# The autocorrelation's shifted sums: two circles of 128 steps in place of one of 255

## The chip, the cores and the metric

The kernel runs on one core of a Trainium2 chip, all in float32. The metric is the device time of one execution in microseconds (us). A profile is one execution seen by the hardware profiler; its times are counted from the first instruction of that execution.

## The reference, cut to what matters

The program is a two-layer decoder for 8 sequences of 128 tokens with 512 features. Layer 0 is causal attention, an autocorrelation with a second input (the context), and a feed-forward part with low-rank experts; layer 1 has attention, cross-attention and another feed-forward part. Each sublayer ends in a residual and a normalization. The change is in layer 0's autocorrelation, whose keys and values are both the context:

```python
qf = jnp.fft.fft(q, axis=2)
kf = jnp.fft.fft(k, axis=2)
corr = jnp.fft.ifft(qf * jnp.conj(kf), axis=2).real
topk = int(C * np.log(L))                       # 9 of 128 shifts, per feature
w, idx = jax.lax.top_k(corr.transpose(0, 1, 3, 2), topk)
w = jax.nn.softmax(w, axis=-1)
for i in range(topk):
    g = jnp.minimum(idx[:, :, None, :, i] + pos, L - 1)
    out = out + w[:, :, None, :, i] * jnp.take_along_axis(v, g, axis=2)
```

So for each feature there is a correlation over 128 shifts on a circle, a choice of the nine largest with softmax weights, and a sum of the values shifted by those amounts. A shift does not wrap round here: past the end, the last token is repeated.

## The kernel before, in words

Batch elements go through layer 0 in four pairs. Causal attention runs in 16 steps `n` (four pairs times four groups of heads, `f`). A step computes scores (`s_a`, line 165), adds the mask (`e_a`, line 370), takes maxima (`m_a`) and exponentials (line 194, ScalarE), turns the probabilities of the step before (`pt_a`, `pT_a`), multiplies out the step before that (`o_a`) and makes the next step's queries and keys (`pq`, `pk`). The output projection of a finished pair (`projection`, `po`) is spread over steps of the next.

The autocorrelation of a pair is the class `Correlated`, cut into pieces:

- `spectra`: real transforms of the tokens (`pa`) and the context (`pb`) by matmul with a table, 64 frequencies by cosine and sine; the two elements of the pair take 64 output partitions each. ScalarE copies pa to `xa`; VectorE multiplies (`pr`), GpSimd adds.
- `correlate`: back to 128 shifts (`pc`), copied to `co`.
- `chosen(h)`: for element `h` of the pair, the nine largest per feature by max and match_replace on VectorE (`top`, `nxt`, `wk1`, `wk2`), softmax weights `ex`.
- `shifted(h)`: the weights are turned (`pt_wT`, `wT`); the context (`pvf`) and the weights (`pw`) go to the spectrum of a circle of 255, long enough that no shift wraps; ScalarE copies pw to `wf`; VectorE forms the products (`vw`), GpSimd their sum and difference.
- `done(h)`: back to 128 positions (`poc`), residual and normalization.

The pieces of pairs 0 and 1 are laid into attention steps by the dictionary `beside`, beginning with step 7 for pair 0 and step 11 for pair 1, at two places in each step (`auto(n, 0)`, `auto(n, 1)`). Pair 2 begins after the last attention step; its rest, and pair 3, lie among the expert stage's pieces by an order written out by hand at lines 716 to 761 (`T`, `R` and `E` turn tokens, route them, and sum the experts). A scheduler puts the instructions on each engine, so the order on an engine is close to the text but not the same. Each engine works through its own queue in order.

PSUM is handed out by two pools: `bank` (four single banks) and `banks` (two double ones). The score and turning tiles of attention, and pa, pb, pc, pvf and pw, are double ones. Context tiles (`ct`) have four buffers, filled by `context(p)` on SP's queue: pairs 0 and 1 at the start, the others at the end of steps 11 and 15. The transform tables lie side by side in one tile, `dft`; T_A is the 128-circle, T_V and T_W the 255-circle of the context and of the weights, T_I and T_J the ways back.

Of the kernel before, what the change touches and what calls it, by code (L numbers as in the profile page):

```python
# [29 lines left out]


C_CAUSAL, C_HEAD = 0, 3 * P
C_SIGN = 3 * P + 2
N_MASK = 3 * P + 3
T_A, T_I, T_W, T_V, T_J = 0, P, 3 * P, 5 * P, 7 * P
N_DFT = 9 * P


# [5 lines left out]
def decoder(ctx: ExitStack, tc: tile.TileContext, a: dict, out: bass.AP):  # L44
# [15 lines left out]
    def banks(name):  # L60
        return ps2.tile([P, 2, 512], F32, tag="ps2", name=name)
# [17 lines left out]
    causal = masks[:, C_CAUSAL : C_CAUSAL + 3 * P]  # L79
    pair = masks[:, C_HEAD : C_HEAD + 2]  # L80
    sign = masks[:, C_SIGN : C_SIGN + 1]

    def mm_acc(ps, pairs):
        n = len(pairs)
# [222 lines left out]

    def context(p):
        for b in (2 * p, 2 * p + 1):
            cts[b] = cp.tile([P, D], F32, tag="ct", name=f"ct_{b}", bufs=4)  # L310
            nc.sync.dma_start(cts[b], a["ctx"][b])

    wq, wq_parts = by_columns("L0_Wq")
# [17 lines left out]
        xs[b] = xp.tile([P, D], F32, tag="x", name=f"x_in_{b}")  # L331
        nc.sync.dma_start(xs[b], a["x"][b])
    nc.sync.dma_start(dft, a["dft"])
    for p in range(2):
        context(p)
    wbase = weight4("F0_base")
    wlora = weight("F0_lora")
    w1q = weight4("L1_Wq")
# [30 lines left out]
    def causal_bias(e, s, r0):  # L369
        return nc.vector.tensor_tensor(e, s, bc(causal.unsqueeze(1), [P, 2, 3 * P]), ALU.add)  # L370

    def projection(b, oT):
        po = bank(f"po0_{b}")
        mm_acc(po, [(oT[:, b % 2, c, :], wo[:, c, :]) for c in range(NC)])
        nc.gpsimd.tensor_tensor(xs[b], xs[b], bqkv[:, 1, :], ALU.add)
        xs[b] = add_norm(xs[b], po, f"a0_{b}", late)


    def swapped(t):

        return t[:, 1:3, :]

    class Correlated:
# [5 lines left out]
        def spectra(self):  # L389

            ps = {}
            for n, src in (("a", xs), ("b", cts)):
                ps[n] = banks(f"p{n}_{self.p}")
                for i in range(2):
                    for h, b in enumerate(self.bs):
                        nc.tensor.matmul(
                            ps[n][64 * h : 64 * h + 64, i, :],
                            lhsT=dft[:, T_A + 64 * i : T_A + 64 * i + 64], rhs=src[b], start=True, stop=True,
                        )
                if n == "a":  # L400
                    xa = cp.tile([P, 3, D], F32, tag="sp", name=f"xa_{self.p}", bufs=2)
# [23 lines left out]
        def chosen(self, h):  # L425

            b, co = self.bs[h], self.co[:, h]

            top = sm.tile([P, NC, 8], F32, tag="top", name=f"top_{b}")
            nxt = sm.tile([P, NC, 8], F32, tag="nxt", name=f"nxt_{b}")  # L430
            wk1 = cp.tile([P, NC, P], F32, tag="wk1", name=f"wk1_{b}")
            wk2 = cp.tile([P, NC, P], F32, tag="wk2", name=f"wk2_{b}")
            for i in range(NC):
                nc.vector.max(top[:, i, :], co[:, i, :])
                nc.vector.match_replace(wk1[:, i, :], top[:, i, :], co[:, i, :], BIG)
                nc.vector.max(nxt[:, i, :], wk1[:, i, :])

            nc.vector.memset(nxt[:, :, TOPK - 8 :], BIG)
            for i in range(NC):
                nc.vector.match_replace(wk2[:, i, :], nxt[:, i, :], wk1[:, i, :], BIG)  # L440
# [3 lines left out]
            nc.vector.scalar_tensor_tensor(ex, wk2, BIG, ex, ALU.is_equal, ALU.mult)  # L444
            su = sm.tile([P, NC], F32, tag="su", name=f"su_{b}")
            nc.vector.tensor_reduce(su, ex, AX.X, ALU.add)
            rc = sm.tile([P, NC], F32, tag="rcw", name=f"rcw_{b}")
            nc.vector.reciprocal(rc, su)
            nc.gpsimd.tensor_tensor(ex, ex, bc(rc.unsqueeze(2), [P, NC, P]), ALU.mult)
            self.ex[h] = ex  # L450

        def shifted(self, h):
            b = self.bs[h]
            wT = cp.tile([P, NC, P], F32, tag="wT", name=f"wT_{b}")
            transposed(self.ex[h].rearrange("p c t -> p (c t)"), NC, P, wT, f"wT_{b}", "a")
            pv = banks(f"pvf_{b}")
            pw = banks(f"pw_{b}")
            for i in range(2):
                nc.tensor.matmul(
                    pv[:, i, :], lhsT=dft[:, T_V + i * P : T_V + (i + 1) * P], rhs=cts[b], start=True, stop=True  # L460
                )
# [11 lines left out]
            nc.vector.tensor_tensor(vw[1], pv, swapped(wf), ALU.mult)  # L473
            nc.gpsimd.tensor_tensor(vw[1][:, 0, :], vw[1][:, 1, :], vw[1][:, 0, :], ALU.subtract)
            self.ri[h] = [t[:, 0, :] for t in vw]

        def done(self, h):
# [22 lines left out]
    beside = {}  # L500
    for p in range(2):
        for i, pieces in enumerate(autos_of[p].pieces()):
            beside.setdefault((begun + NC * p + i // 2, i % 2), []).extend(pieces)

    def auto(n, place):
        for piece in beside.pop((n, place), []):
# [8 lines left out]
    for n, (p, f) in enumerate(steps):  # L515
# [215 lines left out]
    E(1)  # L731
    T(3)
    third.done(1)
    fourth.correlate()
# [1 line left out]
    fourth.chosen(0)  # L736
    E(2)
    T(4)
    R(4)
    fourth.shifted(0)  # L740
    fourth.chosen(1)
# [2 lines left out]
    xT = turned_tokens(0)  # L744
    fourth.done(0)
    R(5)
    E(4)
    fourth.shifted(1)
    raw = [normed(i, 0, xT) for i in range(2)]
# [443 lines left out]
def _mask_table():  # L1193
# [3 lines left out]
    t[:, C_CAUSAL : C_CAUSAL + 3 * P] = np.concatenate([half, half])  # L1197
    t[:, C_HEAD : C_HEAD + 2] = (np.arange(P)[:, None] // HD) % 2 == np.arange(2)
    t[:, C_SIGN] = np.where(np.arange(P) % 64 == 0, -1.0, 1.0)
    return t  # L1200


# [11 lines left out]
def _dft_table():  # L1214
# [10 lines left out]
    cos, sin = waves(S, s, f)  # L1225
    cos[:, 0], sin[:, 0] = even, odd
    t[:, T_A : T_A + 64], t[:, T_A + 64 : T_A + P] = cos, sin
    cos, sin = waves(S, f, s)
    cos[0], sin[0] = even, odd
    for n, part in enumerate((cos, sin)):  # L1230
        t[:, T_I + n * P :][:, :P] = np.concatenate([2 * part / S] * 2)

    n = 2 * S - 1
    cos, sin = waves(n, np.arange(n), s)
    t[:, T_W : T_W + P], t[:, T_W + P : T_W + 2 * P] = cos[:S], sin[:S]
    for i, whole in enumerate((cos, sin)):

        t[: S - 1, T_V + i * P :][:, :P] = whole[: S - 1]
        t[S - 1, T_V + i * P :][:P] = whole[S - 1 :].sum(0)
    c = np.where(s == 0, 1.0, 2.0)[:, None] / n  # L1240
    cos, sin = waves(n, s, s)
    t[:, T_J : T_J + P], t[:, T_J + P : T_J + 2 * P] = c * cos, c * sin
    return t.astype(np.float32)


# [77 lines left out]
```

## Time and profile before

| | us |
|---|---|
| median of 3 runs | 889.24 (888.7 to 889.26) |
| the profiled execution | 888.51 |
| its span, first to last instruction | 886.7 |
| TensorE busy | 852.5 |
| VectorE busy | 562.8 |
| ScalarE busy | 370.2 |
| GpSimd busy | 189.0 |

The profiled execution takes 1.8 us more than its span, and lies 0.7 us under the median. PE is TensorE (PEld its weight loads), DVE is VectorE, ACT is ScalarE, POOL is GpSimd and SP issues most DMAs. One float32 matmul appears as two records. In the groups and timelines a line has its start, its duration, the engine, the line of the kernel, the operation, what is written and read, and in square brackets the idle time before it and who ended that. Stages by time: layer 0's attention with pairs 0 and 1 of the autocorrelation until about 225 us, the experts with pairs 2 and 3 until about 345, then layer 1.

### The profile page before, as it was taken

Reading aid. Unit: us, or ns where it says so; the run is one execution under the profiler, and the core shown is the slowest. Engines: PE = TensorE matmul, PEld = TensorE weight load, DVE = VectorE, ACT = ScalarE, POOL = GpSimd, SP = SyncE. Lnnn points to the kernel's source line nnn. Section 1 sums busy time; section 2 is a strip of 40 time slices with the busy share of each in tenths; the row PEclk is TensorE's granted clock in tenths of the full one; section 3 lists DMA queues with packets and bytes.
Section 4 is the critical chain, followed back from the end, with each engine's and each line's share of the span. In section 5 each row is a group of like instructions: output and inputs, shape, how many; then the busy total and the mean of one; then the engine's idle time right before and its main releaser. Section 6 shows DMA issues by size and latency. Waiting matters only on the chain.

```text
span 886.7 us, 16971 instructions
## 1 busy us (share of the span) xinstructions
PE 852.5 (96%) x6454; PEld 524.6 (59%) x6454; DVE 562.8 (63%) x1329; ACT 370.2 (42%) x1534; POOL 189.0 (21%) x267
## 2 busy tenths in 40 slices
PE   9999999999899999999999999999999999999996
PEld 5766655754445454555555688758475846576442
DVE  3756797776968658788888621735363545467654
ACT  3787474564222116766666603213122322224310
POOL 2400233132243224555555300000000000000000
PEclk9999999999999999999999999999999999999998
DMA  9800000130300002000004020332113211313340
GB/s 331 322 2 25 2 13 13 49 108 1 131 0 25 1 0 96 2 1 2 2 1 143 27 72 1 70 89 45 41 36 92 45 47 36 82 42 78 83 94 35
DMA packets 30067, 50.68 MB, mean 57 GB/s; under 512 B 5537, under 2 KB 22049, under 8 KB 28193
## 3 DMA queue, kind: packets, MB, share of 16 engines
q1 hardware_dynamic: 27424, 47.49, 18.0%
q10 hardware_dynamic: 2560, 2.10, 1.1%
q8 instruction: 51, 0.84, 0.4%
q14 instruction: 32, 0.25, 0.1%
HBM read 30.69 MB, written 2.10 MB: 37 GB/s over the span
## 4 chain that ended last, share of the span: by engine, by line
PE 63%; DVE 20%; ACT 11%; POOL 2%; issue 1%; DMA 1%; SPq 0%; ACTq 0%; POOLq 0%; DVEq 0%
PE pqx L86 9%; PE pox L974 8%; ACT e_a L194 7%; PE pkx L86 4%; PE pvx L86 4%; PE s_x L912 4%; PE pof L86 4%; PE o_x L957 4%; PE pq L86 3%; PE pk L86 3%; DVE e_a L703 3%; PE pv L86 3%; DVE m_a L182 3%; PE pt_a L225 2%; PE pw L463 1%
## 5 line engine op out<-in xcount | busy, mean ns | idle before, releaser
L194 ACT ACTIVATE e_a<-e_a,m_a 128x128 f32<-128x128 f32 (+1 forms) x512 | 184.7, 364 | 93.6 <-DVE m_a L182 93.6
L933 ACT ACTIVATE e_x<-s_x,m_x 128x256 f32<-128x256 f32 x128 | 58.7, 484 | 140.2 <-DVE m_x L923 122.8
L194 ACT ACTIVATION_READ_ACCUMULATOR e_a<-e_a,m_a 128x1 f32 x512 | 96.8, 189 | 0.0
L974 PE MATMUL pox<-w_X_o,oTx 128*128 128x512 f32 x192 | 84.9, 596 | 1.0 <-DVE oTx L963 1.0
L86 PE MATMUL pqx<-xTx,w_X_q 128*128 128x256 f32 x384 | 84.9, 380 | 0.0
L86 PEld LDWEIGHTS pqx<-xTx,w_X_q 128*128 128x128 f32 x384 | 72.6, 190 | 11.4 <-issue 1.8
L922 DVE TENSOR_REDUCE m_x<-s_x 128x4 f32<-128x1024 f32 x32 | 37.6, 1217 | 41.2 <-PE s_x L912 41.2
L974 PEld LDWEIGHTS pox<-w_X_o,oTx 128*128 128x128 f32 x192 | 35.7, 190 | 46.4 <-issue 44.3
L182 DVE TENSOR_REDUCE m_a<-e_a 128x4 f32<-128x512 f32 (+1 forms) x128 | 62.6, 541 | 0.0
L97 POOL TENSOR_TENSOR rs_x<-ve_x,neghalf 128x1 f32<-128x1 f32 x7 | 3.8, 549 | 269.4 <-DVE ve_x L95 250.4
L208 POOL TENSOR_TENSOR e_a<-e_a,rc_a 128x512 f32<-128x512 f32 x64 | 51.8, 827 | 44.0 <-DVE rc_a L205 19.9
L225 PE MATMUL pt_a<-ident,e_a 128*128 128x128 f32 x384 | 48.7, 274 | 4.9 <-DVE e_a L370 3.9
L225 PEld LDWEIGHTS pt_a<-ident,e_a 128*128 128x128 f32 x384 | 43.4, 140 | 12.9 <-DVE e_a L370 4.9
L912 PE MATMUL s_x<-kTx,qTx 32*128 32x256 f32 x768 | 50.0, 385 | 1.0 <-ACT e_x L933 1.0
L912 PEld LDWEIGHTS s_x<-kTx,qTx 32*128 32x128 f32 x768 | 39.0, 184 | 17.1 <-issue 11.7
L957 PE MATMUL o_x<-pT_x,vx 128*32 128x512 f32 x384 | 43.7, 595 | 1.8 <-issue 0.6
L941 DVE STREAM_TRANSPOSE e_x<-e_x 128x1024 f32<-128x1024 f32 x32 | 39.7, 1241 | 0.8
L940 DVE TENSOR_SCALAR e_x<-e_x,rc_x 128x256 f32<-128x256 f32 x128 | 36.3, 347 | 4.2 <-DVE rc_x L937 2.5
L103 DVE TENSOR_TENSOR x_x<-pox,x_a 128x512 f32<-128x512 f32 x7 | 4.8, 686 | 52.5 <-PE pox L974 52.5
L823 ACT COPY qTx<-pqx 128x512 f32<-128x512 f32 x24 | 14.1, 595 | 55.5 <-PE pqx L86 55.5
L165 PEld LDWEIGHTS s_a<-kbd,qT 32*64 32x64 f32 x1024 | 20.7, 131 | 27.7 <-issue 12.7
L165 PE MATMUL s_a<-kbd,qT 32*64 32x256 f32 (+1 forms) x1024 | 33.2, 335 | 2.1 <-DVE pT_a L226 1.1
(223 smaller groups left out, 1611.8 us busy)
## 6 DMA issues: line engine op xcount, KB each, us to landing
pT_x<-e_x SPq DMA_DIRECT2D x224, 64.0 KB, 2.0
w_X_q<-in_X_q SPq DMA_DIRECT2D x3, 1024.0 KB, 4.8
w_X_o<-in_X_o SPq DMA_DIRECT2D x3, 1024.0 KB, 4.7
w_L_Wv<-in_L_Wv SPq DMA_DIRECT2D x2, 1024.0 KB, 6.3
w_L_Wo<-in_L_Wo SPq DMA_DIRECT2D x2, 1024.0 KB, 7.5
x_in<-in_x SPq DMA_DIRECT2D x8, 256.0 KB, 8.2
ct<-in_ctx SPq DMA_DIRECT2D x8, 256.0 KB, 4.4
cT<-in_ctxT SPq DMA_DIRECT2D x4, 512.0 KB, 4.0
```

The source lines that it names most:

```text
L86: nc.tensor.matmul(ps, lhsT=l, rhs=r, start=(i == 0), stop=(i == n - 1))
L165: nc.tensor.matmul(s[r // 2][64 * u : 64 * u + 64, r % 2, cols], lhsT=qT[rows, 64 - 64 * part : P - 64 * part], rhs=kbd[rows, :, :keys], s ...
L182: self.scored = nc.vector.tensor_reduce(self.m[:, part, rs, :], self.by_heads(part)[:, rs], AX.X, ALU.max, negate=True)
L194: nc.scalar.activation(e[:, r, x, :], e[:, r, x, :], AF.Exp, bias=self.m[:, part, r, x : x + 1], accum_out=self.su[:, part, r, x : x + 1],)
L208: nc.gpsimd.tensor_tensor(e, e, bc(self.rc[:, part, rs, :].unsqueeze(3), list(e.shape)), ALU.mult)
L225: nc.tensor.transpose(pt[:, r, cols], self.e[:, 2 * i + r, cols], ident)
L912: nc.tensor.matmul(sc[g // 2][:, g % 2, u * 256 : (u + 1) * 256], lhsT=qT[rows, (h0 + u) * NS + n, :], rhs=kT[rows, n], start=(n == 0), st ...
L922: nc.vector.tensor_reduce(m, self.s[i], AX.X, ALU.max, negate=True)
L933: nc.scalar.activation(self.e[:, :, j, :], self.s[half][:, i, :].rearrange("p (a k) -> p a k", k=32), AF.Exp, bias=self.m[:, j : j + 1], s ...
L941: nc.vector.transpose(self.e[:, :, js, :], self.e[:, :, js, :])
L957: nc.tensor.matmul(po[32 * g : 32 * g + 32, :], lhsT=v[:, s, g * XD + 32 * n : g * XD + 32 * n + 32], rhs=pT[:, s].rearrange("p i h x -> p ...
L974: nc.tensor.matmul(po, lhsT=oT[:, n, h * P : (h + 1) * P], rhs=w, start=(i == 0), stop=(i == NX - 1))
```

## The change

The sum of shifted values is computed on two circles of 128 steps, the usual one and one on which the sign changes at each turn; together they hold what a circle of 256 holds. On the first, the context's spectrum is the one that `spectra` has made for the correlation (its table, now T_B, counts the last token 64 times more at frequency 0, which shifts all correlations of a feature alike). ScalarE copies it from PSUM to rows 0 to 63 of a new tile `vf`, one for each element. The second circle's spectrum comes from a new piece, `other_circle`, with 64 columns for each element, and is copied to rows 64 to 127. GpSimd makes a third plane of vf, in which row 0 has its sign turned. In `shifted` only the weights are transformed, and VectorE multiplies them out of PSUM with vf; the copies to wf are gone. `shifted` is split in two: `turned` (the turn of the weights) and the rest, which for pairs 0 and 1 lies in the middle of an output projection. There are now three places in a step, and thirteen pieces. Context tiles have two buffers, and `context(1)` moves from the start to the end of step 7. match_replace works in place, without wk2.

```diff
+T_A, T_B, T_N, T_I, T_W, T_J = 0, P, 2 * P, 3 * P, 5 * P, 7 * P
...
-            cts[b] = cp.tile([P, D], F32, tag="ct", name=f"ct_{b}", bufs=4)
+            cts[b] = cp.tile([P, D], F32, tag="ct", name=f"ct_{b}", bufs=2)
...
-    for p in range(2):
-        context(p)
+    context(0)
...
-    def projection(b, oT):
+    def projection(b, oT, between=lambda: None):
         po = bank(f"po0_{b}")
-        mm_acc(po, [(oT[:, b % 2, c, :], wo[:, c, :]) for c in range(NC)])
+        for c in range(NC):
+            nc.tensor.matmul(po, lhsT=oT[:, b % 2, c, :], rhs=wo[:, c, :], start=(c == 0), stop=(c == NC - 1))
+            if c == 1:
+                between()
...
+            self.vf = [cp.tile([P, 3, D], F32, tag="vf", name=f"vf_{b}", bufs=2) for b in self.bs]
+            for h in range(2):
+                nc.scalar.copy(self.vf[h][:64, 0:2, :], ps["b"][64 * h : 64 * h + 64])
+
+        def other_circle(self):
+            for i in range(2):
+                pn = bank(f"pn_{self.p}_{i}")
+                for h, b in enumerate(self.bs):
+                    nc.tensor.matmul(
+                        pn[64 * h : 64 * h + 64, :],
+                        lhsT=dft[:, T_N + 64 * i : T_N + 64 * i + 64], rhs=cts[b], start=True, stop=True,
+                    )
+                for h in range(2):
+                    nc.scalar.copy(self.vf[h][64:, i, :], pn[64 * h : 64 * h + 64])
+            for h in range(2):
+                nc.gpsimd.tensor_scalar(self.vf[h][:, 2, :], self.vf[h][:, 0, :], sign0, None, ALU.mult)
...
+        def turned(self, h):
+            self.wT = cp.tile([P, NC, P], F32, tag="wT", name=f"wT_{self.bs[h]}")
+            transposed(self.ex[h].rearrange("p c t -> p (c t)"), NC, P, self.wT, f"wT_{self.bs[h]}", "a")
+
         def shifted(self, h):
-            b = self.bs[h]
-            wT = cp.tile([P, NC, P], F32, tag="wT", name=f"wT_{b}")
-            transposed(self.ex[h].rearrange("p c t -> p (c t)"), NC, P, wT, f"wT_{b}", "a")
-            pv = banks(f"pvf_{b}")
+            b, vf = self.bs[h], self.vf[h]
             pw = banks(f"pw_{b}")
             for i in range(2):
                 nc.tensor.matmul(
-                    pv[:, i, :], lhsT=dft[:, T_V + i * P : T_V + (i + 1) * P], rhs=cts[b], start=True, stop=True
+                    pw[:, i, :], lhsT=dft[:, T_W + i * P : T_W + (i + 1) * P],
+                    rhs=self.wT.rearrange("p c t -> p (c t)"), start=True, stop=True,
                 )
-            for i in range(2):
-                nc.tensor.matmul(
-                    pw[:, i, :], lhsT=dft[:, T_W + i * P : T_W + (i + 1) * P],
-                    rhs=wT.rearrange("p c t -> p (c t)"), start=True, stop=True,
-                )
-            wf = cp.tile([P, 3, D], F32, tag="sp", name=f"wf_{b}", bufs=2)
-            nc.scalar.copy(wf[:, 0:2, :], pw)
-            nc.scalar.copy(wf[:, 2, :], pw[:, 0, :])
...
-            nc.vector.tensor_tensor(vw[0], pv, wf[:, 0:2, :], ALU.mult)
+            nc.vector.tensor_tensor(vw[0], pw, vf[:, 0:2, :], ALU.mult)
...
-                [self.spectra], [],
-                [self.correlate], [lambda: self.chosen(0)],
-                [lambda: self.shifted(0)], [lambda: self.chosen(1)],
-                [lambda: self.done(0), lambda: self.shifted(1)], [],
+                [self.spectra], [], [self.other_circle],
+                [self.correlate], [], [lambda: self.chosen(0)],
+                [lambda: self.turned(0)], [lambda: self.shifted(0)], [lambda: self.chosen(1)],
+                [lambda: self.done(0), lambda: self.turned(1)], [lambda: self.shifted(1)], [],
                 [lambda: self.done(1)],
...
-            projection(2 * p - 3 + f, oTs[p - 1])
+            projection(2 * p - 3 + f, oTs[p - 1], lambda: auto(n, 1))
...
-        auto(n, 1)
-        if n > begun and f == NC - 1:
+        auto(n, 2)
+        if n >= begun and f == NC - 1:
             context(n // NC)
...
     autos_of[2].correlate()
+    autos_of[2].other_circle()
     catch_up()
...
     T(1)
+    third.turned(0)
     R(1)
     third.shifted(0)
...
     third.done(0)
+    third.turned(1)
     R(2)
     third.shifted(1)
     fourth.spectra()
     E(1)
+    fourth.other_circle()
     T(3)
     third.done(1)
```

The fourth pair's `turned` pieces are moved ahead of a routing or an expert sum in the same way.

More of the change, by code (lines that the diff above doesn't have):

```diff
@@ L32 @@
 C_CAUSAL, C_HEAD = 0, 3 * P
-C_SIGN = 3 * P + 2
-N_MASK = 3 * P + 3
-T_A, T_I, T_W, T_V, T_J = 0, P, 3 * P, 5 * P, 7 * P
+C_SIGN, C_SIGN0 = 3 * P + 2, 3 * P + 3
+N_MASK = 3 * P + 4
+T_A, T_B, T_N, T_I, T_W, T_J = 0, P, 2 * P, 3 * P, 5 * P, 7 * P
 N_DFT = 9 * P
@@ L81, in decoder @@
     sign = masks[:, C_SIGN : C_SIGN + 1]
+    sign0 = masks[:, C_SIGN0 : C_SIGN0 + 1]
     def mm_acc(ps, pairs):
@@ L391, in spectra @@
             ps = {}
-            for n, src in (("a", xs), ("b", cts)):
+            for n, src, table in (("a", xs, T_A), ("b", cts, T_B)):
                 ps[n] = banks(f"p{n}_{self.p}")
@@ L397, in spectra @@
                             ps[n][64 * h : 64 * h + 64, i, :],
-                            lhsT=dft[:, T_A + 64 * i : T_A + 64 * i + 64], rhs=src[b], start=True, stop=True,
+                            lhsT=dft[:, table + 64 * i : table + 64 * i + 64], rhs=src[b], start=True, stop=True,
                         )
                 if n == "a":
-                    xa = cp.tile([P, 3, D], F32, tag="sp", name=f"xa_{self.p}", bufs=2)
+                    xa = cp.tile([P, 3, D], F32, tag="sp", name=f"xa_{self.p}", bufs=1)
                     nc.scalar.copy(xa[:, 0:2, :], ps[n])
@@ L431, in chosen @@
             wk1 = cp.tile([P, NC, P], F32, tag="wk1", name=f"wk1_{b}")
-            wk2 = cp.tile([P, NC, P], F32, tag="wk2", name=f"wk2_{b}")
             for i in range(NC):
@@ L439, in chosen @@
             for i in range(NC):
-                nc.vector.match_replace(wk2[:, i, :], nxt[:, i, :], wk1[:, i, :], BIG)
+                nc.vector.match_replace(wk1[:, i, :], nxt[:, i, :], wk1[:, i, :], BIG)
             ex = cp.tile([P, NC, P], F32, tag="ex", name=f"ex_{b}", bufs=2)
@@ L443, in chosen @@
             nc.scalar.activation(ex, ex, AF.Exp)
-            nc.vector.scalar_tensor_tensor(ex, wk2, BIG, ex, ALU.is_equal, ALU.mult)
+            nc.vector.scalar_tensor_tensor(ex, wk1, BIG, ex, ALU.is_equal, ALU.mult)
             su = sm.tile([P, NC], F32, tag="su", name=f"su_{b}")
@@ L459, in shifted @@
                 nc.tensor.matmul(
-                    pv[:, i, :], lhsT=dft[:, T_V + i * P : T_V + (i + 1) * P], rhs=cts[b], start=True, stop=True
-                )
-            for i in range(2):
-                nc.tensor.matmul(
-                    pw[:, i, :], lhsT=dft[:, T_W + i * P : T_W + (i + 1) * P],
-                    rhs=wT.rearrange("p c t -> p (c t)"), start=True, stop=True,
-                )
-            wf = cp.tile([P, 3, D], F32, tag="sp", name=f"wf_{b}", bufs=2)
-            nc.scalar.copy(wf[:, 0:2, :], pw)
-            nc.scalar.copy(wf[:, 2, :], pw[:, 0, :])
+                    pw[:, i, :], lhsT=dft[:, T_W + i * P : T_W + (i + 1) * P],
+                    rhs=self.wT.rearrange("p c t -> p (c t)"), start=True, stop=True,
+                )
             vw = [cp.tile([P, 2, D], F32, tag="prod", name=f"vw_{b}_{i}", bufs=3) for i in range(2)]
-            nc.vector.tensor_tensor(vw[0], pv, wf[:, 0:2, :], ALU.mult)
+            nc.vector.tensor_tensor(vw[0], pw, vf[:, 0:2, :], ALU.mult)
             nc.gpsimd.tensor_tensor(vw[0][:, 0, :], vw[0][:, 0, :], vw[0][:, 1, :], ALU.add)
-            nc.vector.tensor_tensor(vw[1], pv, swapped(wf), ALU.mult)
-            nc.gpsimd.tensor_tensor(vw[1][:, 0, :], vw[1][:, 1, :], vw[1][:, 0, :], ALU.subtract)
+            nc.vector.tensor_tensor(vw[1], pw, swapped(vf), ALU.mult)
+            nc.gpsimd.tensor_tensor(vw[1][:, 0, :], vw[1][:, 0, :], vw[1][:, 1, :], ALU.subtract)
             self.ri[h] = [t[:, 0, :] for t in vw]
@@ L502, in decoder @@
         for i, pieces in enumerate(autos_of[p].pieces()):
-            beside.setdefault((begun + NC * p + i // 2, i % 2), []).extend(pieces)
+            if pieces:
+                beside.setdefault((begun + NC * p + i // 3, i % 3), []).extend(pieces)
     def auto(n, place):
@@ L738, in decoder @@
     T(4)
+    fourth.turned(0)
     R(4)
@@ L746, in decoder @@
     R(5)
+    fourth.turned(1)
     E(4)
@@ L1199, in _mask_table @@
     t[:, C_SIGN] = np.where(np.arange(P) % 64 == 0, -1.0, 1.0)
+    t[:, C_SIGN0] = np.where(np.arange(P) == 0, -1.0, 1.0)
     return t
@@ L1227, in _dft_table @@
     t[:, T_A : T_A + 64], t[:, T_A + 64 : T_A + P] = cos, sin
+    ncos, nsin = waves(2 * S, s, 2 * f + 1)
+    t[:, T_W : T_W + P] = np.concatenate([cos, ncos], axis=1)
+    t[:, T_W + P : T_W + 2 * P] = np.concatenate([sin, nsin], axis=1)
+    bcos, bsin = cos.copy(), sin.copy()
+    bcos[S - 1, 0] += S // 2
+    bsin[S - 1, 0] += S // 2
+    t[:, T_B : T_B + 64], t[:, T_B + 64 : T_B + P] = bcos, bsin
+    for i, part in enumerate((ncos, nsin)):
+        part = part.copy()
+        part[S - 1] -= part.sum(0)
+        t[:, T_N + 64 * i :][:, :64] = part
     cos, sin = waves(S, f, s)
     cos[0], sin[0] = even, odd
-    for n, part in enumerate((cos, sin)):
+    ncos, nsin = waves(2 * S, 2 * f + 1, s)
+    for n, (part, other) in enumerate(((cos, ncos), (sin, nsin))):
         t[:, T_I + n * P :][:, :P] = np.concatenate([2 * part / S] * 2)
[L1233 to L1242, printed above, removed]
+        t[:, T_J + n * P :][:, :P] = np.concatenate([part / S, other / S])
     return t.astype(np.float32)
```

## The prediction

> **What bounds the kernel now.** I read the page first, for the engines' shares, then busy time by stretch around the change, the chain of waits there, and the timelines of TensorE, ScalarE, VectorE and GpSimd.
>
> ```profile
> span 886.7 us, 16971 instructions
> PE 852.5 (96%) x6454; PEld 524.6 (59%) x6454; DVE 562.8 (63%) x1329; ACT 370.2 (42%) x1534; POOL 189.0 (21%) x267
> ```
>
> TensorE is busy for 96% of the span, so matmul time taken away should shorten it, except where something else sets the pace. Hence the stretches (columns: PE, PEld, DVE, ACT, POOL busy, granted clock, DMA):
>
> ```profile
> 85.50:93.60 8.10, 8.07 (x103) 3.50 (x103) 4.07 (x5) 4.18 (x16) 3.33 (x5) 1.00 0.01 2
> 106.00:124.20 18.20, 15.65 (x134) 9.53 (x130) 17.71 (x59) 10.29 (x40) 7.62 (x9) 1.00 0.06 16
> 124.20:140.40 16.20, 16.20 (x143) 10.08 (x135) 12.40 (x23) 9.14 (x38) 4.15 (x5) 1.00 0.06 17
> 168.60:187.60 19.00, 16.91 (x134) 10.71 (x131) 17.93 (x60) 10.29 (x40) 7.61 (x9) 0.91 0.19 64
> 225.20:238.00 12.80, 9.18 (x66) 6.84 (x65) 12.02 (x63) 3.91 (x9) 3.67 (x7) 1.00 0.59 226
> 238.00:282.00 44.00, 42.64 (x164) 22.01 (x165) 34.13 (x130) 12.61 (x25) 15.43 (x16) 1.00 0.00 1
> 282.00:345.00 63.00, 62.23 (x245) 31.68 (x243) 41.09 (x104) 16.17 (x56) 18.06 (x23) 1.00 0.11 36
> ```
>
> The first line is attention step 7 (pair 0's spectra): TensorE full. 106 to 124 (steps 8 and 9, the first selection and shifted sum) and 225 to 238 belong to VectorE: 17.71 of 18.20 and 12.02 of 12.80 us. 124 to 140 (step 10) and 282 to 345 are TensorE again. So the same matmul has a different worth in each place. The chain of waits has the two matmul forms in question:
>
> ```profile
> 131.64 1.72 PE pvf L459 x4
> ...
> 149.18 1.72 PE pb L396 x8
> ```
>
> A matmul appears as two records. The context's 255-circle spectrum (two 128-column matmuls) takes 1.72 us per batch element. Four 64-column matmuls, two elements side by side, also take 1.72: for a pair the narrow form costs half.
>
> **The change, part by part.** *TensorE.* Removed: pvf, 8 x 1.72 = 13.8 us. Added: `other_circle`, 4 pairs x 1.72 = 6.9. The narrow form has a price at its borders: pair 1's spectra begin at 147.25 and the next matmul starts at 150.83, 3.58 us for 16 records x 0.215 = 3.44; before them poc at 145.44 + 1.72 should have freed TensorE at 147.16, not 147.25. Together 0.23 us, so one `other_circle` costs 1.95.
>
> *ScalarE.* Removed per pair: the wf copies, 2 x (1.01 + 0.59) = 3.2 us. Added: two 64x1024 copies of pb and four 64x512 copies of pn. No 64-partition copy is shown. Upper value: the full-height rows (1.01 and 0.59), 4.4 us. Lower: half, 2.2. I take the upper, since the 112x256 copy (0.38) and the 128x256 one (0.37) do not differ by height. Its cover in step 7 is this gap:
>
> ```profile
> 95.34 0.40 ACT L194 ACTIVATE e_a<-e_a,m_a 128x128 f32<-128x128 f32 x1 [5.66 <-DVE m_a L182]
> ```
>
> ScalarE is free from 89.7 to 95.3 (7.1 us in step 11, 10 us before 227.3). pb is ready at 89.1 and pn at about 93.6; pushed down by pn's own 1.95, the exps start at 97.3. The copies fit with some 1.6 us to spare: cost zero. Without the cover they push the exps, and through them `co` and the selection, by up to 4.4.
>
> *VectorE.* The two products per element are the same size (PSUM x SBUF, 1.22 and 1.21); in-place match_replace costs the same. They no longer wait for wf, a step of 1.0 to 1.6 us from pw to product.
>
> *PSUM.* pv no longer holds a double bank. Before, the score matmuls of the next step waited for it:
>
> ```profile
> 122.61 0.88 PE L165 MATMUL s_a<-kbd,qT 32*64 32x256 f32 x22 [0.21 <-DVE vw L473]
> ```
>
> The 32 records from 121.55 took 1.87 us in place of 0.91, so 0.96 was lost (0.95 in step 13). But pw still holds a bank until the second product is done, so the recovery lies between 0 and 1.0 per pair. Against it, pvf covered the wT copy (ends 116.03); now two projection matmuls do, ending near 115.6, so pw may wait 0.4. I set these off as zero.
>
> *GpSimd.* Two `tensor_scalar` 128x512 per pair are new. Lower bound: memset of that size, 0.53. Upper: two-tensor add, 1.27. I take 1.04, the add with a broadcast operand: 8.3 us in all, beside 189 busy of 887. On the path only if just ahead of a norm's rs (0.55), `ex`, or the fourth pair's subtraction (264.92). There is also the shared port:
>
> ```profile
> 224.39 1.89 DVE L107 TENSOR_SCALAR x_a<-x_a,mv_a,rs_a 128x512 f32<-128x512 f32 x1 [0.66 <-POOL rs_a L97]
> 224.75 0.53 POOL L270 MEMSET vd<- 128x512 f32 x1
> ```
>
> This normalization takes 0.55 us elsewhere; beside GpSimd's memsets it took 1.89. The Trainium skill (SBUF — State Buffer, "Who interferes with whom") states why: VectorE's two-port `tensor_scalar` and GpSimd share a port pair, and whoever comes second is fully blocked. Were each of the eight new passes to block a VectorE instruction on the path, that would be +8.3 us and turn the sum to about +3. But in 92 to 104 VectorE runs reductions and sums out of PSUM, with no normalization to meet; only the two expert pairs have some near. I take 0.7 us in all for queue and port, ends 0 and 8.3.
>
> *SP's queue.* Context pair 1 moves from the start to the end of step 7 (about 95 us; used at 149), pair 2 to step 11 (about 153; used at 215), pair 3 behind the third `other_circle` (about 229; used at 257). A load lands in 4.4 us, so nothing waits. Queued behind pair 3 are w_X_v and the alibi table, first used after 330. Cost zero; a late load would stall spectra by at most the landing time, 4.4. Only two ct buffers remain, but their last reader is now `other_circle`, not the late shifted sum. xa and vf have free slots by then. The 0.5 MB less at the start only helps loads already early.
>
> **The sum**, by place:
> - Pairs 0 and 1: +1.95 in step 7 (11), where TensorE is full. In step 9 (13), -1.72: VectorE is the busier, but TensorE runs unbroken from 112.3 apart from the waits above, and VectorE's selection of the second element can finish later. In step 10 (14), -1.72. Net -1.5 each, -3.0.
> - Pair 2: `other_circle` takes the place of the first pvf at 227.7, in the stretch where TensorE has 3.6 us idle: 0. The second pvf (249.5): -1.7.
> - Pair 3: +1.95 near 260, ahead of `done(1)`, which frees the buffer for the second product (263.6) and so sets the correlation. The first pvf (275 to 279) fills around gaps (0.35 and 0.60): about -0.8 of 1.72. The second (297.3): -1.72. Net -0.6.
> - GpSimd: +0.7.
>
> Total -4.6 us. From the profiled execution's 888.51 that gives 883.9; the median of 889.24 lies 0.73 above it, so against the median 884.6.
>
> **Rivals.**
> 1. *The sum as above*: 884.6, own range 882.5 to 887. Chance 0.52.
> 2. *The waits go too.* Products start without wf and the score banks come free: another 1.0 for each pair of the attention and 1.0 in the expert stage, with the 0.7 on GpSimd unseen: 4.6 + 3.0 + 0.7 = 8.3, so 880.9. For: the 0.96 us lost at 121.6 and 184.9. Against: VectorE is 97% busy there. Chance 0.2.
> 3. *Gain lost.* VectorE sets steps 8 and 9 so strictly that their pvf is worth nothing: 3.4 less gain, 888.0, within 0.2%. For: 17.71 of 18.20. Against: TensorE's own row of work after 112.3. Chance 0.12.
> 4. *ScalarE's new copies miss their gap, slower.* If pn runs so late that its copies come in order among the exps of step 8 (95.3 to 102.4, back to back, followed at once by `co`, from which the VectorE stretch hangs), each pair pays up to 4.4; 3.5 each for pairs 0 and 1 is +7.0 on -4.6: +2.4, so 891.6. It decides from about 1.6 us of lateness. For: instructions do not run in the text's order (step 7's values matmuls are split around the spectra). Against: the 5.66 us gap. Chance 0.16.
>
> That the narrow matmuls do not overlap would cost 6.9 more and end at 891.5, but pb shows that they do.
>
> **How the numbers follow.** Predicted 884.6, the likeliest. A further spread of 1.7 is the clock: in the stretch from 168.6 to 187.6 it was 0.91, which cost 19.0 x 0.09 = 1.7 us, while the like stretch from 106 had 1.00. The range 880 to 891 takes in cases 1 to 3 and the milder half of 4. About 0.2% (1.8 us) is what a measurement can tell from no change. Faster: nearly all of 1 and 2, 0.71. Same: 3 and a little of 1, 0.12. Slower: 4 and a remainder, 0.17.
>
> **What would show it.** TensorE's busy time falls by about 6, to 846.5; the pvf and wf groups are gone; a pn group shows 32 records in 4 x 1.72 us. Step 7 grows by 1.95, steps 9 and 10 shrink by 1.7 each; 225 to 238 keeps its length. s_a's wait for vw stays or shrinks. ScalarE's exps of step 8 start at most 2 us later. Wrong if those exps start over 3.5 us later, if VectorE's normalizations grow beside the new GpSimd passes, if spectra wait for ct, or if time moves after 345, which the change does not touch.

## The result: slower by half a per cent, and the profile after

| | before | after |
|---|---|---|
| median of six runs each, us | 888.97 (888.1 to 890.89) | 894.03 (892.9 to 895.02) |
| the profiled execution, us | 888.51 | 894.21 |
| ratio of after to before | | 1.0055, interval 1.0042 to 1.0068 |

The kernel became 5.1 us slower; 4.6 us faster was predicted. Line numbers move by a few: the shared matmul helper is L87 in place of L86, pw L479 in place of L463, the products vw L484 and L486, pn L422. From the page of after, the span and each engine's busy time with its share of the span:

```profile
span 892.4 us, 16987 instructions
PE 852.2 (95%) x6454; PEld 523.2 (59%) x6454; DVE 562.7 (63%) x1329; ACT 375.7 (42%) x1542; POOL 200.7 (22%) x275
```

By the prediction's count some 6 us of matmul work is gone, yet TensorE's busy time fell by only 0.3: part of what is left ran at a lower clock (the run *gate first* below does the same work in 848.3). Busy time by stretch in after (PE, PEld, DVE, ACT, POOL busy, granted clock, DMA), for attention steps 7 and 10 and two stretches of the expert stage:

```profile
79.30:96.00 16.70, 16.07 (x151) 8.86 (x143) 10.72 (x18) 12.26 (x42) 5.08 (x7) 1.00 0.04 7
125.90:142.10 16.20, 15.20 (x134) 9.34 (x130) 13.81 (x26) 7.65 (x36) 5.06 (x6) 1.00 0.00 1
238.00:243.00 5.00, 4.39 (x14) 3.46 (x15) 3.34 (x24) 1.04 (x4) 0.79 (x2) 0.66 0.00 0
284.00:288.00 4.00, 3.85 (x13) 3.31 (x14) 2.68 (x16) 0.70 (x2) 0.62 (x2) 0.63 0.00 0
```

Step 7 is TensorE-bound as before and has grown. Step 10, which was 16.20 of 16.20 on TensorE before, now has 1.0 us of idle TensorE and is no shorter. At 238 and 284 the clock is 0.66 and 0.63, where before had 1.00 in all of 225 to 345.

Where the 5.70 us of the two spans lie, by stages that end at the same instruction in both (an output matmul o_a for the first two, a group of score matmuls of layer 1 for the third). The start differs before anything that the change computes; it lay between 77.6 and 80.3 us in the profiles of all runs here:

| stage (us) | before | after | difference | predicted |
|---|---|---|---|---|
| start, to the head of step 7 | 77.97 | 78.52 | +0.55 | 0 |
| attention with pairs 0 and 1 | 139.38 | 140.45 | +1.07 | -3.0 |
| experts with pairs 2 and 3 | 126.97 | 131.21 | +4.24 | -1.6 |
| layer 1 | 542.38 | 542.22 | -0.16 | 0 |

The attention by steps, each from its first query matmul pq to that of the next (the last two columns are experiments below; step 14, whose next step begins otherwise, is measured between output matmuls and went from 16.12 to 16.27):

| step | before | after | predicted change | candidate | pick ahead |
|---|---|---|---|---|---|
| 7 / 11 (other_circle) | 14.75 / 15.76 | 16.66 / 17.62 | +1.95 each | 16.65 / 17.62 | 16.66 / 17.62 |
| 9 / 13 (first pvf out) | 18.26 / 18.95 | 17.45 / 16.79 | -1.72 each | 17.21 / 16.76 | 17.80 / 17.83 |
| 10 (second pvf out) | 16.12 | 16.27 | -1.72 | 15.90 | 14.20 |

Steps 7 and 11 grew by what was predicted (why, the run with the circle moved will show), steps 9 and 13 together gave 3.0 of the 3.4 us, and steps 10 and 14 gave nothing. Each of the two profiles has one stretch of low clock in these steps, before in step 13 and after in step 9, so in the sum they cancel. One lengthens its step by about 0.7 us: 18.95 us against 18.26 for the same step without it (in the run *before, with the transposes early*), and 17.45 against 16.79. The larger loss is in the experts. TensorE's timeline there, first before (start, duration, instruction; in brackets the idle time and what ended it):

```profile
227.70 1.88 PE L459 MATMUL pvf<-ct,dft 128*128 128x512 f32 x4
229.42 1.86 PE L86 MATMUL pg<-w_F_lora,xTf 128*128 128x252 f32 x8
231.12 0.60 PE L129 MATMUL pt_xTf<-ident,x_c 128*128 128x128 f32 x4
233.37 1.97 PE L86 MATMUL pg<-w_F_lora,xTf 128*128 128x252 f32 x8 [1.65 <-ACT xTf L139]
236.63 0.66 PE L129 MATMUL pt_wT<-ident,ex 128*128 128x128 f32 x4 [1.29 <-POOL ex L449]
```

and after:

```profile
228.82 1.94 PE L422 MATMUL pn<-ct,dft 128*64 128x512 f32 x8
230.69 0.66 PE L130 MATMUL pt_xTf<-ident,x_c 128*128 128x128 f32 x4
233.01 1.97 PE L87 MATMUL pg<-w_F_lora,xTf 128*128 128x252 f32 x8 [1.66 <-ACT xTf L140]
234.81 0.60 PE L130 MATMUL pt_xTf<-ident,x_c 128*128 128x128 f32 x4
238.61 0.66 PE L130 MATMUL pt_wT<-ident,ex 128*128 128x128 f32 x4 [3.19 <-POOL ex L468]
239.10 3.52 PE L87 MATMUL pg<-w_F_lora,xTf 128*128 128x252 f32 x8
...
284.15 1.12 PE L130 MATMUL pt_wT<-ident,ex 128*128 128x128 f32 x4 [3.78 <-POOL ex L468]
285.06 2.79 PE L87 MATMUL pg<-w_F_lora,xTf 128*128 128x252 f32 x8
```

The second group of pg (the gate of the next tokens) stood ahead of the wait for ex before, and stands behind it after. It needs nothing of ex, but TensorE works its list in order. Twice the wait is over 3 us, and twice the pg behind it takes 3.52 or 2.79 us where 1.97 is its full-speed time.

### The profile page after: what moved, and what is told of

Its sections match the earlier page's. It is cut to its first block, busy times and chain, and to the rows that moved or that the text cites. A ratio compares the mean times of both kernels' runs of the same rounds, so it can differ in the third digit from the quotient of the medians.

```text
span 892.4 us, 16987 instructions
## 1 busy us (share of the span) xinstructions
PE 852.2 (95%) x6454; PEld 523.2 (59%) x6454; DVE 562.7 (63%) x1329; ACT 375.7 (42%) x1542; POOL 200.7 (22%) x275
## 4 chain that ended last, share of the span: by engine, by line
PE 59%; DVE 22%; ACT 13%; POOL 3%; issue 1%; DMA 1%; SPq 0%; ACTq 0%; POOLq 0%; DVEq 0%
PE pqx L87 9%; ACT e_a L195 9%; PE pox L995 8%; PE pkx L87 4%; PE pvx L87 4%; PE pof L87 4%; PE s_x L933 4%; PE o_x L978 4%; DVE m_a L183 3%; DVE e_a L719 3%; PE pq L87 3%; PE pv L87 2%; PE pk L87 2%; PE pg L87 1%; DVE e_a L370 1%
## 5 line engine op out<-in xcount | busy, mean ns | idle before, releaser
L87 PE MATMUL pqx<-xTx,w_X_q 128*128 128x256 f32 x384 | 84.9, 380 | 0.0
L87 PEld LDWEIGHTS pqx<-xTx,w_X_q 128*128 128x128 f32 x384 | 72.6, 190 | 11.4 <-issue 1.8
```

Of the source, the lines that this page charges most:

```text
L87: nc.tensor.matmul(ps, lhsT=l, rhs=r, start=(i == 0), stop=(i == n - 1))
```

## The experiments

**First batch: is it GpSimd, the amount of TensorE work, or the place of that work?** In the texts on record, P is the theory of the sign passes, F that of missing fillers and clock.

*The sign passes left out.* Of after:

```diff
-            for h in range(2):
-                nc.gpsimd.tensor_scalar(self.vf[h][:, 2, :], self.vf[h][:, 0, :], sign0, None, ALU.mult)
-            nc.vector.tensor_tensor(vw[1], pw, swapped(vf), ALU.mult)
+            nc.vector.tensor_tensor(vw[1], pw, vf[:, 0:2, :], ALU.mult)
```

> The changed kernel without GpSimd's two passes per pair that make vf's third plane; the second product reads planes 0 and 1, so the sign of frequency 0 is left out of the sums. The passes took 1.57 us each, 12.5 us in all. Theory P (they cost: GpSimd's queue ahead of ex in the expert stage, and the port that VectorE shares): 2 to 4 us faster than the changed kernel, 890 to 892. Theory F (what costs is where TensorE's work stands: the second circle is added where TensorE is full, the context's old spectrum was taken from where it filled waits): about 1 us faster at most, 893; TensorE's idle of 3.2 us before the third pair's turned weights shrinks by no more than 1.

Measured: 892.46 us, 1.0037 of before (1.0023 to 1.0051). That lies between what the two theories expected. The waits for ex went from 3.19 and 3.78 us to 2.73 and 3.76. By the medians the passes cost some 1.6 us, under a third of the loss (the intervals of this run and of after overlap); they are not its main cause.

*Two matmuls with no purpose in each wait.* Of after (`filler` makes two 128x512 matmuls whose result nobody reads):

```diff
+    filler("fill_3")
     third.turned(0)
...
+    filler("fill_4")
     fourth.turned(0)
```

> The changed kernel with two 128x512 matmuls that nobody reads, before turned(0) of the third and of the fourth pair, where the old spectrum pvf used to fill TensorE's wait for the selection: 3.4 us of TensorE work added. Theory F with the clock [...]: the waits of 3.2 and 3.8 us are half filled, the clock stays at 1.00 after them, and the time falls by 1 to 3 us in spite of the added work, 891 to 893. A theory in which TensorE's volume decides: 3.4 us slower, 897.5. If idle without the clock: no change, 894.

Measured: 892.02 us, 1.0034 (1.0019 to 1.0049): more work and, by the medians, 2.0 us less time. TensorE's timeline of this run:

```profile
237.91 0.66 PE L130 MATMUL pt_wT<-ident,ex 128*128 128x128 f32 x4 [1.52 <-POOL ex L468]
238.40 1.87 PE L87 MATMUL pg<-w_F_lora,xTf 128*128 128x252 f32 x8
...
281.76 0.72 PE L130 MATMUL pt_wT<-ident,ex 128*128 128x128 f32 x4 [2.06 <-POOL ex L468]
282.27 3.53 PE L87 MATMUL pg<-w_F_lora,xTf 128*128 128x252 f32 x8
```

With 1.52 us of idleness pg ran at full speed; with 2.06, half filled, it still took 3.53, so the expectation of a clock of 1.00 held behind one wait of two. The idle time itself costs a second time, through the clock. The amount of work is refuted as the cause.

*The circle moved into the waits.* other_circle of pairs 0 and 1 at steps 9 and 13 instead of 7 and 11, that of pairs 2 and 3 just ahead of turned(0):

```diff
-                [self.spectra], [], [self.other_circle],
+                [self.spectra], [], [],
...
+        if n in (9, 13):
+            autos_of[(n - 9) // 4].other_circle()
...
+    third.other_circle()
     third.turned(0)
```

> The changed kernel with the second circle's matmuls (and the next context load) moved: for pairs 0 and 1 to steps 9 and 13 ahead of the turning of the probabilities, where TensorE waits 2 us for VectorE's selection; for pairs 2 and 3 between chosen(0) and turned(0), where it waits 3.2 to 3.8 us. Nothing is added or removed. Theory F: 1.95 us come back in each of four places, and the clock with them in the last two: 7 to 10 us faster than the changed kernel, 884 to 887, thus faster than the kernel before. Theory P: as the changed kernel, 893 to 894, as GpSimd's passes stay. A rival (the copies of pn out of PSUM, now in the selection's stretch, delay ex or the weights' copy on ScalarE): gain under 4 us.

Measured: 899.0 us, 1.0112 (1.0091 to 1.0132). This expectation failed badly. GpSimd's timeline in the third pair says why:

```profile
237.24 3.12 POOL L429 TENSOR_SCALAR vf<-vf,masks 128x512 f32<-128x512 f32 x2 [1.92 <-ACT vf L427]
240.33 1.04 POOL L468 TENSOR_TENSOR ex<-ex,rcw 128x512 f32<-128x512 f32 x1
```

The filler brought its own followers: the two sign passes, which wait for ScalarE's copies of pn, came into GpSimd's queue just ahead of the division of ex, for which TensorE waits. That wait grew to 5.05 us. In steps 9 and 13 TensorE also stood idle for 1.23 and 1.92 us ahead of the second half of pn, until VectorE was done with the output oT (that pn waits there for the PSUM bank which this frees is inferred). A matmul without successors fills a wait; this one lengthened it.

The run shows one thing more. With other_circle gone from steps 7 and 11 they are still 16.42 and 16.82 us long, against 14.75 and 15.76 in before. TensorE's timeline in step 7, first before, then this run:

```profile
91.88 0.91 PE L165 MATMUL s_a<-kbd,qT 32*64 32x256 f32 x32
```

```profile
93.79 0.88 PE L166 MATMUL s_a<-kbd,qT 32*64 32x256 f32 x16 [0.60 <-ACT vf L416]
```

The second half of the score matmuls waits for ScalarE's copies of pb into vf, which are new and keep pb's double bank until 93.7, and the two halves run one after the other in place of side by side. In after, pn fills this time. So of the 1.91 and 1.86 us in steps 7 and 11 only 0.24 and 0.80 leave with the matmuls of pn.

*No other circle at all.* The matmuls of pn and their copies are left out, and both halves of vf are filled from pb:

```diff
-                nc.scalar.copy(self.vf[h][:64, 0:2, :], ps["b"][64 * h : 64 * h + 64])
+                nc.scalar.copy(self.vf[h][:, 0:2, :], ps["b"])
```

> The changed kernel without the second circle at all: no pn matmuls and no pn copies; vf is filled from pb at full height, so its rows 64 to 127 hold the wrong spectrum. 6.9 us of TensorE work less, 7.8 with its borders. TensorE's volume decides: 7.8 us faster, 886. Theory F: steps 7 and 11 give back 1.95 each, but in the expert stage the third pair's circle stood in a wait of TensorE (0 to 0.5 us) and the fourth's on the chain (up to 1.95): 4 to 6 us faster, 888 to 890, and the waits before the turned weights stay or grow.

Measured: 891.94 us, 1.0031 (1.0023 to 1.004), a smaller gain than either theory expected: 7.8 us of TensorE work less than after brought 2.1. The waits for ex grew to 5.97 and 5.41 us, so in the experts everything taken out came back as idle time (131.1 us after 131.2). The attention took 137.48 us in place of 140.45. Steps 7 and 11 gave only 0.3 and 0.9 us, since there too the score matmuls wait for the copies of pb (0.53 us in step 7, by vf L416). Step 9 gave 1.5, about 0.7 of it the stretch of low clock that after's profile has there (0.57 in 116 to 120) and this one has not.

**Second batch: the order.** F had named the waits but not what made them. Comparing the order of TensorE's instructions in the two kernels showed the exchange seen above. Two runs test it from both sides.

*Gate first*, of after:

```diff
-    third.turned(0)
     R(1)
+    third.turned(0)
...
-    fourth.turned(0)
     R(4)
+    fourth.turned(0)
```

> The kernel after with two calls exchanged in the expert stage: the gate's route(1) is emitted before third.turned(0), and route(4) before fourth.turned(0), as their order was before the change. The same work in all. Theory O (order): the change put the transposes of ex ahead of the gate's matmuls pg (1.97 us), and TensorE runs its list in order, so pg stands behind a wait it used to fill. Then the waits of 3.19 and 3.78 us fall to about 1.3 and 1.9, the low clock behind each (0.63 to 0.66, 1.7 us lost each time) goes, and the copy of wT is less well covered (+0.7 each): about 5.5 us less than after, 888 to 889.5, and 225 to 345 at a clock of 1.00. Rival S (supply): ex comes late because ScalarE's copies of pn and GpSimd's sign passes stand ahead of it, and the order on TensorE matters little: pg moves in but ex stays the limit and the clock falls all the same, 892 to 894.

Measured: 887.96 us, 0.9989 (0.9982 to 0.9996). TensorE's timeline and the same two stretches:

```profile
235.36 1.97 PE L87 MATMUL pg<-w_F_lora,xTf 128*128 128x252 f32 x8 [0.73 <-ACT xTf L140]
237.87 0.66 PE L130 MATMUL pt_wT<-ident,ex 128*128 128x128 f32 x4 [0.54 <-POOL ex L468]
...
281.18 0.66 PE L130 MATMUL pt_wT<-ident,ex 128*128 128x128 f32 x4 [0.59 <-POOL ex L468]
```

```profile
238.00:243.00 5.00, 4.02 (x14) 2.08 (x15) 4.94 (x31) 1.08 (x3) 0.02 (x1) 1.00 0.02 5
284.00:288.00 4.00, 4.00 (x11) 1.80 (x10) 3.93 (x14) 0.00 (x0) 1.15 (x1) 1.00 0.01 2
```

The waits fell to 0.54 and 0.59 us, the clock is 1.00, and the expert stage fell from 131.21 to 125.99 us, with the same work. About 3.4 of these 5.2 us are the two stretches of low clock (1.7 each, worked out in the last section), the rest idle time. TensorE's busy time in the whole run is 848.3. The copies of pn and the sign passes are unchanged here, so rival S falls as the main cause.

*Before, with the transposes early*: the one exchange, in the kernel before, with pvf and all else kept.

```diff
+    third.turned(0)
     R(1)
     third.shifted(0)
...
+    fourth.turned(0)
     R(4)
     fourth.shifted(0)
```

> The kernel before with that one piece of the change alone: the transposes of ex are split from shifted, and third.turned(0) and fourth.turned(0) are emitted ahead of route(1) and route(4). pvf, the 255-circle and all else stay as before, and so does the amount of work. Theory O expects the waits for ex to grow by the 1.97 us of pg that moves behind them (1.29 to about 3.2 in the third pair, under 1 to about 2.5 in the fourth), and a stretch of low clock behind the longer one: slower than before by 3 to 6 us, 892 to 895. Rival S expects no change within 1 us, since neither the copies of pn nor the sign passes are in it.

Measured: 893.29 us, 1.0045 (1.0029 to 1.006). TensorE's timeline:

```profile
236.46 1.11 PE L129 MATMUL pt_wT<-ident,ex 128*128 128x128 f32 x4 [4.91 <-POOL ex L449]
237.37 3.57 PE L86 MATMUL pg<-w_F_lora,xTf 128*128 128x252 f32 x8
```

The exchange alone makes before as slow as after: the expert stage takes 133.07 us, 6.1 more than before's 126.97. The third pair's wait of 4.91 is longer than expected (3.2), and the numbers say why: in before pg stood between two short idle times, 1.65 and 1.29 us; with pg gone from between they merge, 1.65 + 1.97 + 1.29 = 4.91. In after it is the same sum: gate first has 0.73 + 1.97 + 0.54 = 3.24, after 3.19 in one piece. The sum holds for the fourth pair of after too: gate first has 1.22 + 1.97 + 0.59 = 3.78, after 3.78. In this run the fourth pair's wait is 2.04. So the order of two calls in each of the two pairs is worth 5 to 6 us of the stage in either kernel, and is shown, not argued, to be the cause of the loss in the experts.

*Candidate*: gate first, and two more edits.

```diff
-                [lambda: self.done(0), lambda: self.turned(1)], [lambda: self.shifted(1)], [],
+                [lambda: self.turned(1), lambda: self.done(0), lambda: self.shifted(1)], [], [],
...
-                nc.gpsimd.tensor_scalar(self.vf[h][:, 2, :], self.vf[h][:, 0, :], sign0, None, ALU.mult)
+                nc.gpsimd.tensor_tensor(self.vf[h][:, 2, :], self.vf[h][:, 0, :], bc(sign0, [P, D]), ALU.mult)
```

> The run above with gate first, and two more edits. (a) In attention steps 10 and 14 the second element's transposes come first, then the inverse transform of the first element (poc), then pw at once, and both halves of the projection behind it. (b) GpSimd's sign pass is a product with a broadcast operand in place of a tensor_scalar with a per-partition scalar. Expected: (a) the three waits of step 10 in after (poc 0.41, pw 0.36, the score matmuls held back by vw 0.99) go, so steps 10 and 14 fall from 16.27 to about 14.6 us each, which is the 1.72 of pvf that the prediction expected there; if VectorE's or ScalarE's row of work sets that step instead, they stay at 16.1 to 16.3. (b) the pass falls from 1.57 to about 1.04 us, worth at most 1 us in all. Sum with gate first: 885 to 886.5 by the first reading, 888 to 889 by the second.

Measured: 886.73 us, 0.9974 (0.9963 to 0.9984). The sign pass fell from 1.57 to 1.04 us; the experts went from 125.99 to 125.44. Step 10 is 15.90 us, between the two readings (14.6 and 16.1) and nearer the second: the score matmuls are no longer held back, but the first two waits of step 10 remain (0.40 and 0.36 us). Something else still gates that step.

**Third batch: what sets step 10?** *Short pick*: the candidate, and in a second run the kernel before, without the last round of match_replace for the second element of pairs 0 and 1:

```diff
-            for i in range(NC):
+            for i in range(NC if not (h and self.p < 2) else 0):
                 nc.vector.match_replace(wk1[:, i, :], nxt[:, i, :], wk1[:, i, :], BIG)
```

> The candidate with less VectorE work in the attention: for the second element of pairs 0 and 1 the last round of the selection (the four match_replace of the line that takes the ninth value, 1.05 us from 119.90 to 120.95 in the profile of after) is left out, so that element keeps eight shifts. TensorE's work is unchanged. Theory V (in steps 9, 10, 13 and 14 of after VectorE's row of work, unbroken from 110 to 132, sets the end, which is why taking pvf away there brought nothing in steps 10 and 14): steps 9 and 10 together fall by 0.8 to 1.1 us against the candidate, steps 13 and 14 likewise, 1.6 to 2.2 in all. Rival T (TensorE's row sets them, and the waits in it come from ScalarE's copies and from banks): less than 0.3 a pair.

> The kernel before with the same four match_replace left out for the second elements of pairs 0 and 1. There TensorE runs unbroken from 112.3 to 121.5 and through step 10, with pvf in both. Theory V expects little here, since TensorE's pvf covers VectorE's row: at most the 0.96 us that the score matmuls lose to vw in step 9, and nothing in step 10; 0 to 1.9 us in all, and less than in the run above. Rival T expects the same small gain in both runs.

Measured: 887.26 us, 0.9980 (0.9972 to 0.9987), no gain on the candidate, and 888.53, 0.9998 (0.9990 to 1.0005), no gain on before. Steps 9 and 10 together took 33.1 us with and without the round. Theory V, that the amount of VectorE work sets these steps, falls. VectorE's timeline of the first run shows what became of the time saved:

```profile
119.93 0.25 DVE L216 RECIPROCAL rc_a<-su_a 128x16 f32<-128x16 f32 x1 [0.85 <-ACT e_a L195]
120.76 1.22 DVE L484 TENSOR_TENSOR vw<-pw,vf 128x1024 f32<-128x1024 f32 x1 [0.57 <-PE pw L479]
121.90 1.21 DVE L486 TENSOR_TENSOR vw<-pw,vf 128x1024 f32<-128x1024 f32 x1
123.03 0.68 DVE L104 TENSOR_TENSOR x_a<-po,x_in 128x512 f32<-128x512 f32 x1
123.63 1.49 DVE L463 SCALAR_TENSOR_TENSOR ex<-wk,ex 128x512 f32<-128x512 f32 x1
125.15 0.69 DVE L465 TENSOR_REDUCE su<-ex 128x4 f32<-128x512 f32 x1
125.75 0.95 DVE L370 TENSOR_TENSOR e_a<-s_a,masks 128x768 f32<-128x768 f32 x1
```

It became idle time: 0.85 us ahead of a reciprocal, which waits for ScalarE's exponentials, and 0.57 (0.34 in the candidate) ahead of vw, which waits for pw. Behind vw come the mask and the sum of the second element's ex, 2.1 us, and only then e_a, for which the next exps wait. Before had them the other way round: ex at 118.69, vw at 120.24, and e_a at 123.39 right after the score matmuls.

*Pick ahead*: the candidate with that order restored.

```diff
-                [lambda: self.turned(0)], [lambda: self.shifted(0)], [lambda: self.chosen(1)],
+                [lambda: self.turned(0), lambda: self.chosen(1)], [lambda: self.shifted(0)], [],
```

> The candidate with chosen(1) emitted ahead of shifted(0) in attention steps 9 and 13. VectorE's order changes: the mask and the sum of the second element's ex (0.68 + 0.69 us, but 1.48 + 0.69 where they now stand beside GpSimd's subtraction) go before and between the two products vw, as they did in the kernel before, and no longer stand between the score matmuls and e_a of the next step. Work is the same. The short pick showed that VectorE has slack ahead of vw, where it waits for pw. Theory Q (VectorE's queue order: what stands between vw and e_a sets step 10, not the amount of work): e_a of step 10 starts about 2 us earlier, steps 10 and 14 fall from 15.9 to about 14.6 us, steps 9 and 13 grow by at most 0.9 since vw frees the score bank later; together 0.4 to 1.3 us less a pair, so 884.5 to 886. Rival: ScalarE's copy of wT, or the bank that oT frees, sets step 10: it stays at 15.9, and the longer step 9 makes it 887 to 888.5.

Measured: 885.07 us, 0.9957 (0.9944 to 0.9971), the lowest median of all, though its interval overlaps the candidate's. VectorE's timeline:

```profile
122.97 0.69 DVE L463 SCALAR_TENSOR_TENSOR ex<-wk,ex 128x512 f32<-128x512 f32 x1
123.58 1.22 DVE L484 TENSOR_TENSOR vw<-pw,vf 128x1024 f32<-128x1024 f32 x1
124.71 0.68 DVE L465 TENSOR_REDUCE su<-ex 128x4 f32<-128x512 f32 x1
125.30 1.22 DVE L486 TENSOR_TENSOR vw<-pw,vf 128x1024 f32<-128x1024 f32 x1
126.43 0.17 DVE L467 RECIPROCAL rcw<-su 128x4 f32<-128x4 f32 x1
126.52 0.66 DVE L104 TENSOR_TENSOR x_a<-po,x_in 128x512 f32<-128x512 f32 x1
127.09 1.81 DVE L370 TENSOR_TENSOR e_a<-s_a,masks 128x768 f32<-128x768 f32 x2
```

Step 10 fell from 15.90 to 14.20 us; this is the 1.7 that the prediction had looked for there. Step 9 pays part of it back, 17.21 to 17.80, and step 13 16.76 to 17.83, since the second product frees the score bank later (TensorE waits 1.25 us; the trace puts it down to the reciprocal right behind that product). The candidate's profile has a stretch of low clock in step 9 (0.71 in 116 to 120), which makes that step some 0.45 us longer than its step 13; this profile has none. The steps of pair 1, where neither has one, show the exchange by itself: +1.07 in step 13 and -1.70 in step 14 (from pq to the output matmuls: 15.10 to 13.40), together -0.6. The profiled execution was the slowest of the five, 886.95 us: it spent 80.3 us in the start, 2.4 more than the candidate's, so the gain is read from the steps and the medians, not from the two spans.

## Why the prediction was wrong, point by point

- **The price of the new work** came out right, 1.91 and 1.86 us for 1.95, but by luck: 1.67 and 1.06 of it stay when `other_circle` is moved elsewhere. The sum had no term for pb's double bank, which the new copies hold while the score matmuls wait; pn stands in that wait.
- **ScalarE's cover** held for the exps: the copies of pb started at 92.29, later than thought, since they wait 2.07 us for VectorE's second product of pb, yet those of pn were done by 96.7 and ScalarE still waited 1.03 us before the exps of step 8 at 97.76. Rival 4 did not happen. The cost of zero for these copies held only beside pn, as just said.
- **SP's queue** cost nothing visible, as predicted.
- **"GpSimd +0.7"** was mis-sized. The pass took 1.57 us, above the upper bound of 1.27 drawn from other operations of that size; leaving all eight out lowered the median by 1.6 us. In the third pair two of them lay ahead of ex, which the prediction had named as the dangerous place. The sign that it had named, a normalization that grows beside a pass, came once in after, 0.92 us in place of 0.55, beside the pass from 273.70 to 275.27:

```profile
273.75 0.92 DVE L108 TENSOR_SCALAR x_c<-x_c,mv_c,rs_c 128x512 f32<-128x512 f32 x1 [1.74 <-POOL rs_c L98]
```

- **"In step 9 (13), -1.72"**: 3.0 of 3.4 us arrived. Rival 3, that VectorE allows nothing there, is refuted.
- **"In step 10 (14), -1.72"** is the first step that failed: +0.15. The prediction read TensorE's 16.20 of 16.20 as proof that TensorE set the step. It was busy throughout, but with pvf gone a second row lay just behind: the mask and sum of ex had slid behind vw in VectorE's queue, and waits of 0.41 and 0.36 us and the held score bank took pvf's place on TensorE. Rearranging brought 1.70 us in each of steps 10 and 14, of which steps 9 and 13 gave back 0.6 and 1.07.
- **"I set these off as zero"**, the waits: the lost cover for wT cost 0.36 us in step 10. The score bank held by vw went on costing about 1 us in step 9, and in step 10 it began to: the score matmuls, from their start to the output matmuls, took 0.94 us there in before and 1.70 in after, until pw was put ahead of both projections (1.11).
- **"Pair 2: fills the wait, 0" and "pair 3: net -0.6"** is the step that cost most. The sum followed the added and removed matmuls and never costed the two transposes that the diff moves ahead of route(1) and route(4). Each set takes 0.6 us, but it waits for ex, and 1.97 us of pg was queued behind them. With only that put right, the stage came to -0.98 against the predicted -1.6: the sum was right in kind, and its omission was worth 5.2.
- **The range** ended at 891.0 and took in no clock loss from new idle time, although the prediction knew of the clock as chance spread. In the experts it followed from the change. In the attention the 1.7 us that the prediction gave to a stretch of low clock was too much: its step grew by 0.7.

## What to carry to other kernels

When a diff moves an instruction that waits, list what stood between its old and new place on that engine: all of it now waits too, short idle times merge into a long one, and that can cost more than the work the change saves. Work taken off a full engine is a gain only if the next row, on another engine, is not ordered to fill the same time; look at what stands between the last release and the next needed result in each queue, not at busy shares. A filler is worth its idle time only if its own followers do not enter the queue that ends the wait. And a term that comes out right is not yet shown: take the priced work out, and see whether its time goes with it.

## What the hardware showed that was not expected

- **A short idle stretch of TensorE costs twice.** In the expert stage waits of 2.04 to 5.97 us, eleven in six runs, each brought a stretch at half the clock, of 3.41 us or twice that, during the wait or behind it (0.50 in 236 to 240 of *before, with the transposes early*); single waits of 1.5 to 1.7 us were not. In after the stretches of 4 us from 236 and 240 had 0.89 and 0.68: 4 x 0.11 + 4 x 0.32 = 1.7 us lost, and those from 280 and 284 (0.94 and 0.63) again 1.7. The Trainium skill (TensorE: Matmul & The Clock Gate, Part 1) has the clock at half for at least one window of about 3.4 us after an idle window; half of 3.4 is 1.7, which agrees. That 2.0 us of idle time can suffice is what these runs add.
- **At 2.0 us the place of the wait decides, not only its length.** The low stretches of one profile start whole multiples of 3.413 us apart: in after at 116.26, 239.14 and 283.51, so 122.88 and 44.37 us from one to the next, 36 and 13 times 3.413. Laid on that grid, before's wait from 172.93 to 174.89 lies wholly in the window that ends at 175.56, and the clock is low from there; its wait from 110.35 to 112.31, just as long, is cut by a border at 110.71, and the clock stays. So it was in all profiles of this case: of the waits of 1.82 to 2.09 us, the ten with 1.92 us or more inside one window were followed by a low clock, the fourteen with at most 1.87 inside any window were not. That explains why the attention's waits of 2.0 us cost clock in some executions and not in others.
- **GpSimd's price depends on the form, not only the size**: 128x512 took 1.57 us with a per-partition scalar operand, 1.04 as a product with a broadcast tensor, for the same result.
- **ScalarE's copies do not get cheaper with half the partitions**: 64x1024 took 1.01 us and 64x512 0.58, as at full height.
- **VectorE's scalar_tensor_tensor of ex took 1.48 us in after where it started inside GpSimd's subtraction of the products (124.30 to 125.56) and 0.69 where it did not.** The prediction's fear of the shared port was right in kind, but it hit this instruction in steps 9 and 13, and of the normalizations only one beside a new pass.
